# The last projection's first tiles are made during layer 3's last sums; a first mask, weights' wait, stage ends and first weights of attention at other places

## The chip, the cores and the metric

One core of a Trainium2 chip runs the whole program. The metric is the device time of one execution in microseconds; where several runs were made, their median. A profiled execution gives the trace that the times of single instructions come from.

A core has a TensorE for matrix products (PE; its weight loads are listed apart as PEld), a VectorE (DVE), a ScalarE (ACT), a GpSimd (POOL) and a SyncE (SP). Each engine works through its own list of instructions in a fixed order and waits on semaphores for the others. SP, POOL and ACT also issue DMAs, each in the order of its list: a DMA that has to wait for something holds up those behind it.

## The reference

Four graph layers on 2708 nodes with 512 features, each of the form x = layernorm(x + layer(x, adj)). adj is a symmetric 0/1 matrix with ones on its diagonal, about 2.3% full. Cut to what matters:

```python
def layer0(X, A):                      # at most 64 neighbours of each row
    Ab = A > 0
    keep = Ab & (jnp.cumsum(Ab, axis=1) <= 64)
    cnt = keep.sum(axis=1, keepdims=True)
    xj = leaky_relu((keep @ X / maximum(cnt, 1)) @ W_nb.T + b_nb)
    xi = leaky_relu(X @ W_line.T + b_line)
    return xi + where(cnt > 0, xj, 0)

def layer1(x, adj):
    agg = mask @ x / maximum(deg, 1)
    return relu(concat([x @ W_self + b_self, agg @ W_nb + b_nb]) @ W_comb + b_comb)

def heads(x, mask, W, a):              # 8 heads of 64, or one of 512
    Wh = einsum('nf,hfo->hno', x, W)
    e = leaky_relu((Wh @ a_src)[:, :, None] + (Wh @ a_dst)[:, None, :], 0.2)
    return softmax(where(mask, e, -9e15)) @ Wh

def layer2(x, adj): return heads(x, adj, W, a)          # 8 heads, side by side
def layer3(x, adj):
    x1 = elu(heads(x, adj, W1, a1))                     # 8 heads, side by side
    h2 = elu(heads(x1, adj, Wo, ao))                    # one head of 512
    return relu(h2 @ lin1_w + lin1_b) @ lin2_w + lin2_b
```

## The kernel before

The 2708 rows are NT = 22 tiles of 128 (the last has 20 rows); features are D = 512, so a product with a 512 x 512 weight is KD = 4 steps. The transposed adjacency matrix stays in SBUF as `maskT`, one byte an entry. Most pools are rings: a tile of a name takes the oldest of `bufs` buffers and waits until that one's readers are done. A scheduler orders each engine's instructions by priorities that follow the program text; `tc.issue_after(x)` asks for an instruction to be ordered behind x. `early(ahead, n, make)` makes item i a number of steps before it is used. `ahead`, `late` and `const` are pools that live through the whole fast path.

Stages, in their order, with the lines of the kernel before:

- Layer 0, projections (loop over t at L293 to L324). For each row tile: x is loaded and transposed (L125, L127), multiplied with W_nb (`keep_y`, L223 and L224, splits the product into two parts yH and yL) and with W_line (products at L229). The second one gets its bias (L318) and leaky relu and goes to r0_dram. Meanwhile HERE of the 22 row tiles of adj ("masks") are loaded (L242), counted by a Sigmoid (L247, ACT), scanned so that only 64 neighbours a row stay (`place`: L253 and L256, DVE) and turned (L265, PE) into maskT. The W_line weight is transposed before the loop (L137, L138).
- Layer 0, sums (the loop over blocks of four tiles with L459). 6 blocks of row tiles; each runs over 22 tiles j of y with two products a tile (yH, yL) against `kT`, the mask widened by ACT (L335). Generators are stepped between the products: `both`, once a step, makes the masks that are left (`other_masks`), the weights of layer 1 and small vectors of the attention layers; `todo`, on odd j, runs `finish` of the block before: bias, leaky relu, the addition of r0 and x (both loaded), layer norm, and the store to x1_dram (L384, POOL). A block ends with ACT's scaled copies `u<-acc` (L472).
- Layer 1: its projections (L478 to L491) and sums over the full mask (L505).
- Layers 2 and 3. `project` (products at L608) makes for each row tile R (the features scaled by `ecol`, L622), ucol, vcol and the row v, which goes to v_dram and comes back broadcast over all partitions (`v_bc`, L665). `heads_attention` then makes the sums: two blocks of 11 row tiles (1408 and 1300 columns), four pairs of heads a block, so 8 runs; each run has 22 steps j and each step, for its two heads, one DVE operation for e (L671, max(v, u) times mask), one ACT operation for c (L679, which says where the first branch holds) and PE's products po (L829) and, with c, pd (L744, the divisors). Products of the mask with `parts_m` (L727) belong to the divisors too: 88 for a block, in three portions, then `fold` (L716) and `keep` (L736). For block 0 all are run ahead of the first run; for block 1 during the run before it needs them.
- The output of a run of layer 2 is turned back (L777), copied into a tile `o` (L785) from the ring "xT", and stored to o_dram (L789, L791); layer 3's projection reads it again (`summed`), one tile ahead.
- The output of a run of layer 3 stays transposed and goes to oT_dram (L808); the reciprocals of its divisors are transposed after a block's last pair (`spread`: L795, L797) and stored to rc_dram by eight DMAs on POOL's queue (L799). The projection of the last head (`p4`, L608 again) takes its input from `elu_turned`: loads of oT (L880) and rc (L882), broadcast over the partitions, and then DVE (L884), ACT Exp (L885), DVE (L886, L887) for two tiles at a time; o lies in a part of `lin`, a large tile that is made when the attention's pools are given back.
- The last head's sums (L939 to L973) with the two linear layers, and the layer norm.

`okc` sums counts that must come to `expected`; otherwise a slower general version runs, which does not happen with these inputs.

Of the kernel before, what the change touches and what calls it, by code (L numbers as in the profile page):

```python
# [18 lines left out]
P = 128  # L19
# [11 lines left out]
def kernel(  # L31
# [18 lines left out]
    def rows(t):  # L50
        return min(P, N - t * P)
# [39 lines left out]
    oT_dram = dram.tile([D, N], F32, name="oT_dram")  # L91
    rc_dram = dram.tile([H, NT * P], F32, name="rc_dram")
# [102 lines left out]
    with ExitStack() as phase:  # L195
# [39 lines left out]
        HERE = NT - 7  # L235
# [40 lines left out]
        with ExitStack() as ph:  # L276
# [21 lines left out]
            for t in range(NT):  # L298
# [10 lines left out]
                now = counted < min(HERE, -(-t * HERE // (NT - 4)))  # L309
# [9 lines left out]
                low = leaky(u[:n], u[:n])  # L319
# [8 lines left out]
        with ExitStack() as ph:  # L328
# [9 lines left out]
            def other_masks():  # L338
# [9 lines left out]
                for i in range(HERE, NT):  # L348
# [9 lines left out]
                    for part in range(4):  # L358
                        place(i, m, places, part, 4)
                        yield  # L360
                    psum = (ps_mm.tile([P, G, P], BF16, name=f"pm{k % 2}") for k in range(3))
# [12 lines left out]
            def finish(ts_, us):  # L374
                for t in ts_:
                    n, u = rows(t), us[t]
                    r0, x0 = fetched(r0_dram, t, n), fetched(x, t, n)
# [4 lines left out]
                    nc.vector.tensor_add(u[:n], u[:n], x0)  # L382
# [66 lines left out]
            for i, b in enumerate(cuts):  # L449
                ts_ = range(*b)  # L450
                pa = {t: sums() for t in ts_}
                for j in range(NT):
# [9 lines left out]
                    if j % 2:  # L462
                        next(todo, None)
# [85 lines left out]
    expected = float(P * NT * (3 * H + 1))  # L549
# [10 lines left out]
    def project(name, source, layer, v_dram, cuts, turned=None):  # L560
# [12 lines left out]
        with ExitStack() as ph:  # L573
# [7 lines left out]
            if turned:  # L581
                twos = early(2, -(-NT // 2), lambda i: turned(sm, 2 * i, min(2 * i + 2, NT)))
                xTs = lambda t: twos(t // 2)[:, :, t % 2 * P:t % 2 * P + P]
            vrows, bs = {}, {}
# [14 lines left out]
            for t in range(NT):  # L599
# [19 lines left out]
                for a in range(2):  # L619
                    to, src = R2[:n, t, a * D // 2:(a + 1) * D // 2], pm[a][:n, :D // 2]  # L620
                    if heads > 1:
                        nc.vector.tensor_mul(to.rearrange("p (h o) -> p h o", h=hh),  # L622
# [19 lines left out]
            sq = sm.tile([P, NT, H], F32, name="sq", bufs=1)  # L642
            if heads < H:
                nc.vector.memset(sq, 0.0)
            dd = dcol[:, :, :heads]
            nc.vector.tensor_mul(sq[:, :, :heads], dd, dd)
            sq = sq.rearrange("p t h -> p (t h)")
# [36 lines left out]
    blocks = list(zip(cuts[:-1], cuts[1:]))  # L684

    def heads_attention(name, att, as_rows):
# [3 lines left out]
        with ExitStack() as ph:  # L690
# [56 lines left out]
            def finish(b, h0, p, pair, oT):  # L747
# [3 lines left out]
                feats, cols = slice(h0 * HO, (h0 + 2) * HO), slice(t0 * P, t0 * P + att.width(b))  # L751
# [41 lines left out]
                def spread():  # L793
                    ps = ps_t.tile([P, 512], F32, name="ps_t")
                    pe(nc.tensor.transpose(ps[:12 * H, :P], rcs[:, b].rearrange("p h t -> p (h t)"), ident))  # L795
                    r = sm.tile([12 * H, P], F32, name="r", bufs=1)
                    nc.scalar.copy(r, ps[:12 * H, :P])  # L797
                    for h in range(H):
                        nc.gpsimd.dma_start(rc_dram[h, t0 * P:t1 * P].rearrange("(t p) -> t p", p=P),  # L799
                                          r[12 * h:12 * h + nt])  # L800
# [6 lines left out]
                else:  # L807
                    nc.gpsimd.dma_start(oT_dram[feats, cols], oT.rearrange("p i c -> p (i c)")[:, :att.width(b)])  # L808
# [3 lines left out]

            products, fold, keep = masks(0, pd[1])
            for step in (*products, fold, keep):
                step()
            todo = {}
            for r, (b, h0) in enumerate(runs):
# [23 lines left out]
                todo = finish(b, h0, pd[r % 2], pair, oT)  # L841
# [31 lines left out]

    def elu_turned(sm, t0, t1):

        w = sum(rows(t) for t in range(t0, t1))
        cols = slice(t0 * P, t0 * P + w)
        o = lin[:, -KD * 1024:].rearrange("p (i k n) -> p i k n", i=4, k=KD)[:, t0 // 2 % 4]
        rc = sm.tile([P, KD, 2 * P], F32, name="rc2")
        nc.sync.dma_start(o[:, :, :w], oT_dram.rearrange("(k p) n -> p k n", p=P)[:, :, cols])  # L880
        for q in range(2):
# [460 lines left out]
```

## Time and profile before

| | us |
|---|---|
| three runs: lowest, median, highest | 3063.74, 3064.99, 3065.71 |
| profiled execution: its time | 3066.34 |
| profiled execution: span | 3064.6 |
| layer 0, projections | 0 to 217 |
| layer 0, sums | 217 to 504 |
| layer 1 | 504 to 945 |
| layer 2, projection and sums | to 1548 |
| layer 3, projection and sums | 1556 to 2228 |
| projection of the last head | 2255 to 2338 |
| its sums, linear layers, layer norm | to 3064.6 |

The mean granted TensorE clock is 0.986. In the profile, a line of a timeline has the start, the duration of the group, the engine, the line of the kernel, the operation, its output and inputs, their shapes, how often it ran, and in brackets the idle time ahead of it and what ended that. In a table of stretches, each row has a stretch's bounds and length, then for PE, PEld, DVE, ACT and POOL the busy time and the number of instructions, then the granted clock, the DMA's share and GB/s. This part of the page shows the span in 40 slices of 76.6 us, busy time in tenths:

```profile
PE   7999999999999999999998999999969999999997
DVE  5866649313234999999966999999943535344342
ACT  3556432113224899999955999999932000000001
PEclk9999999999999999999999999999989999999999
```

### The profile page before, as it was taken

To read this page: it belongs to the slowest core of one execution; us is meant where nothing else is said; L and a number is where in the kernel's file an instruction comes from. 1 tells how busy PE (TensorE), PEld (TensorE's weight loads), DVE (VectorE), ACT (ScalarE), POOL (GpSimd) and SP (SyncE) were. 2 spreads that over 40 slices of the span, in tenths; PEclk is the share of its full clock that TensorE was granted. 3 is DMA by queue.
4 is the path that set the end of the run, shared out by engine and by line. 5 is a ranking of instruction groups with operands and counts; after the bars stand their busy time and mean duration, and the time that the engine had idled before them with its cause. 6 is when DMAs were issued, how large, how long until landed. Compare 5 with 4: busy or idle time off the path is not lost. (4 is left out here: it accounts for less than half of the span.)

```text
span 3064.6 us, 36494 instructions
## 1 busy us (share of the span) xinstructions
PE 2918.2 (95%) x14456; PEld 1623.1 (53%) x14456; DVE 2021.9 (66%) x2408; ACT 1545.0 (50%) x1768; POOL 220.9 (7%) x354
## 2 busy tenths in 40 slices
PE   7999999999999999999998999999969999999997
PEld 4447676458887333444465333444356555555565
DVE  5866649313234999999966999999943535344342
ACT  3556432113224899999955999999932000000001
POOL 1110102101110000000022000000000000100001
PEclk9999999999999999999999999999989999999999
DMA  4542343322222000011044000000061000000000
GB/s 124 118 95 59 120 126 112 119 63 90 76 74 80 20 29 29 28 42 34 22 132 128 29 29 28 28 28 27 18 172 48 4 17 14 31 14 15 14 21 20
DMA packets 115972, 174.45 MB, mean 57 GB/s; under 512 B 40062, under 2 KB 63487, under 8 KB 115792
## 3 DMA queue, kind: packets, MB, share of 16 engines
q1 hardware_dynamic: 87120, 110.56, 12.1%
q0 software_dynamic: 18784, 57.79, 6.5%
q10 hardware_dynamic: 9888, 3.67, 0.5%
q8 instruction: 116, 1.90, 0.3%
q14 instruction: 64, 0.52, 0.1%
HBM read 142.01 MB, written 44.64 MB: 61 GB/s over the span
## 5 line engine op out<-in xcount | busy, mean ns | idle before, releaser
L671 DVE SCALAR_TENSOR_TENSOR e<-v_bc,ucol,maskT 128x1300 f32<-128x1300 f32 (+3 forms) x836 | 1181.8, 1474 | 336.7 <-PE pn L973 318.4
L679 ACT ACTIVATE c<-e,bcol 128x1300 fp8e4<-128x1300 f32 (+1 forms) x704 | 994.8, 1424 | 83.2 <-DVE e L671 33.2
L829 PE MATMUL po<-e,R 128*64 128x512 f32 (+2 forms) x4224 | 925.1, 548 | 30.7 <-DVE e L671 28.7
L829 PEld LDWEIGHTS po<-e,R 128*64 128x64 f32 x4224 | 348.6, 136 | 574.6 <-issue 383.7
L973 PE MATMUL pn<-e,R 128*128 128x512 f32 (+1 forms) x1056 | 413.4, 542 | 0.0
L973 PEld LDWEIGHTS pn<-e,R 128*128 128x128 f32 x1056 | 191.1, 190 | 199.2 <-issue 195.9
L941 ACT ACTIVATE w<-pl,b 128x256 f32<-128x256 f32 (+1 forms) x88 | 40.9, 465 | 373.4 <-PE pl L939 373.4
L459 PE MATMUL acc<-yH,kT 128*128 128x512 f32 x484 | 197.3, 408 | 4.3 <-ACT kT L335 4.3
L229 PE MATMUL pm<-w,xT 128*128 128x512 f32 (+1 forms) x384 | 178.7, 609 | 15.2 <-DVE yL L224 9.3
L459 PE MATMUL acc<-yL,kT 128*128 128x512 f32 x484 | 189.8, 392 | 0.0
L505 PE MATMUL acc<-yH,mf 128*128 128x512 f32 x484 | 188.4, 389 | 0.0
L505 PE MATMUL acc<-yL,mf 128*128 128x512 f32 x484 | 188.3, 389 | 0.0
L608 PE MATMUL pm<-w,xT 128*128 128x264 f32 (+1 forms) x704 | 169.5, 395 | 10.5 <-DVE R L622 5.1
L114 POOL TENSOR_TENSOR ln_rs<-ln_rs,half 128x1 f32<-128x1 f32 x88 | 59.2, 673 | 1569.7 <-DVE ln_rs L113 1563.8
L229 PE MATMUL pm<-weight,xT 128*128 128x512 f32 (+1 forms) x352 | 161.7, 602 | 5.9 <-DVE weight L138 5.2
L939 PE MATMUL pl<-lin 128*128 128x256 f32 (+1 forms) x704 | 154.8, 374 | 2.8 <-DVE lin L858 2.8
L948 PE MATMUL pl<-lin,w 128*128 128x512 f32 (+1 forms) x352 | 157.4, 592 | 0.0
L608 PEld LDWEIGHTS pm<-w,xT 128*128 128x128 f32 (+1 forms) x704 | 130.1, 190 | 38.5 <-issue 5.7
L939 PEld LDWEIGHTS pl<-lin 128*128 128x128 f32 x704 | 130.4, 192 | 33.7 <-issue 15.8
L502 ACT CAST mf<-maskT 128x1024 fp32r<-128x1024 fp8e4 (+1 forms) x66 | 64.4, 978 | 158.4 <-PE acc L505 147.9
L223 ACT CAST yH<-pm 128x512 fp32r<-128x512 f32 (+1 forms) x44 | 25.7, 585 | 230.2 <-PE pm L229 230.2
L335 ACT ACTIVATE kT<-maskT 128x512 fp32r<-128x512 fp8e4 (+1 forms) x132 | 77.6, 594 | 118.8 <-PE acc L459 118.7
(198 smaller groups left out, 2690.2 us busy)
## 6 DMA issues: line engine op xcount, KB each, us to landing
rows<-x_dram SPq DMA_DIRECT2D x63, 256.0 KB
v_bc<-v_dram SPq DMA_DIRECT2D x16, 704.0 KB
rows<-in_x_dram SPq DMA_DIRECT2D x42, 256.0 KB
x_dram<-u POOLq DMA_DIRECT2D x42, 256.0 KB, 2.3
v_bc<-v_dram SPq DMA_DIRECT2D x16, 650.0 KB
m<-in_adj_dram POOLq DMA_DIRECT2D x14, 677.0 KB, 6.7
r_dram<-u POOLq DMA_DIRECT2D x21, 256.0 KB, 2.3
rows<-r_dram SPq DMA_DIRECT2D x21, 256.0 KB
```

The costliest lines, as they stand in the source:

```text
L229: order(nc.tensor.matmul(pm[:n], xT[:, k, :n], w[:, k, :], start=(k == 0), stop=(k == KD - 1)))
L335: made = nc.scalar.activation(kT[:, :w], maskT[:, j, b[0] * P:b[0] * P + w], AF.Relu, scale=-1.0)
L459: nc.tensor.matmul(pa[t], kT[:, (t - b[0]) * P:(t - b[0] + 1) * P], y[:, j, :], start=(j == 0 and y is yH), stop=(j == NT - 1 and y is yL))
L502: nc.scalar.copy(mf[:, :g1 - g0, :], maskT[:, g0:g1, t * P:(t + 1) * P])
L505: nc.tensor.matmul(pa, mf[:, j - g0, :], y[:, j, :], start=(j == 0 and y is yH), stop=(j == NT - 1 and y is yL))
L608: nc.tensor.matmul(pm[a][:n, :D // 2 + heads], xT[:, k, :n], w[:, k, a, :D // 2 + heads], start=(k == 0), stop=(k == KD - 1))
L671: nc.vector.scalar_tensor_tensor(e[:, :w], v[:, :w], ucol[:, j, h:h + 1], maskT[:, j, c0:c0 + w], op0=OP.max, op1=OP.mult)
L679: nc.scalar.activation(c[:, :w], e[:, :w], AF.Sigmoid, bias=bcol[:, j, h:h + 1], scale=STEP, saturate=False)
L829: pe(nc.tensor.matmul(po[i][HO * k:HO * k + HO, :c1 - c0], R2[:, j, h * HO:(h + 1) * HO], e[:, c0:c1], start=(j == 0), stop=(j == NT - 1)))
L939: nc.tensor.matmul(pl[:, :w], self.lin1[:, k, f * P:(f + 1) * P], h[:, k, :w], start=(k == 0), stop=(k == KD - 1))
L948: nc.tensor.matmul(pl[:n], gT[:, f, (t - t0) * P:(t - t0) * P + n], self.lin2[:, f, :], start=(f == 0), stop=(f == KF - 1))
L973: nc.tensor.matmul(pn[k][:, :w], R2[:, j, k * P:(k + 1) * P], e[:, :w], start=(j == 0), stop=(j == NT - 1))
```

## The change

- Layer 0, projections: HERE is 14 instead of 15, and the first mask is counted at t = 2 instead of t = 1. x is added to the leaky relu's result right there, before it is stored to r0_dram.
- Layer 0, sums: a mask waits two more steps between its scan and its turn; `finish` no longer loads and adds x; its steps run at two of three j instead of at every second.
- `project`: the last layer's input tiles are cut into three single tiles and then pairs; `sq` holds only the heads that there are; it returns the scaling (L622) of tile 20.
- `heads_attention`: the e's of the first three steps of run 0 are ordered behind that scaling; block 0's products with parts_m, their fold and keep move into run 0 (at j = 12, 16, 20) and to the first steps of run 1.
- The last run's output tiles `o` come from the ring "e" instead of "xT"; `r` comes from the ring "spare".
- oT_dram and rc_dram become one buffer for each block.
- During the last run of layer 3 (in the program's text at j = 9, 13 and 17; the scheduler puts the parts where their inputs allow) `elu_turned` makes tiles 0, 1 and 2 for the last projection, in buffers of the rings "rows", "xT" and "spare". The loads of `elu_turned` are ordered one behind the other.

```diff
-        HERE = NT - 7
+        HERE = NT - 8
...
-                now = counted < min(HERE, -(-t * HERE // (NT - 4)))
+                now = counted < min(HERE, -(-(t - 1) * HERE // (NT - 5)))
...
-                low = leaky(u[:n], u[:n])
+                leaky(u[:n], u[:n])
+                low = nc.vector.tensor_add(u[:n], u[:n], xs(t))
                 nc.gpsimd.dma_start(r0_dram[t * P:t * P + n, :], u[:n])
...
                         place(i, m, places, part, 4)
                         yield
+                    yield
+                    yield
...
-                    r0, x0 = fetched(r0_dram, t, n), fetched(x, t, n)
+                    r0 = fetched(r0_dram, t, n)
...
-                    nc.vector.tensor_add(u[:n], u[:n], x0)
...
-                    if j % 2:
+                    if j % 3:
                         next(todo, None)
...
             if turned:
-                twos = early(2, -(-NT // 2), lambda i: turned(sm, 2 * i, min(2 * i + 2, NT)))
-                xTs = lambda t: twos(t // 2)[:, :, t % 2 * P:t % 2 * P + P]
+                cuts_ = [(t, t + 1) for t in range(3)] + [(t, min(t + 2, NT)) for t in range(3, NT, 2)]
+                parts = early(2, len(cuts_), lambda i: ready[i] if i in ready else turned(sm, *cuts_[i]))
+                xTs = lambda t: parts(t if t < 3 else (t - 3) // 2 + 3)[:, :, ((t - 3) % 2 if t > 2 else 0) * P:][:, :, :P]
...
-                        nc.vector.tensor_mul(to.rearrange("p (h o) -> p h o", h=hh),
+                        scaled[t] = nc.vector.tensor_mul(to.rearrange("p (h o) -> p h o", h=hh),
...
+            return scaled.get(NT - 2)
...
-                    o = ahead.tile([P, KD, P], F32, name="xT")
+                    o = (att.pool.tile([P, att.W], F32, name="e", bufs=5)[:, :KD * P].rearrange("p (t c) -> p t c", t=KD)
+                         if last else ahead.tile([P, KD, P], F32, name="xT"))
...
-                    r = sm.tile([12 * H, P], F32, name="r", bufs=1)
+                    r = late.tile([P, D], F32, name="spare", bufs=2)[:12 * H, :P]
...
-                        nc.gpsimd.dma_start(rc_dram[h, t0 * P:t1 * P].rearrange("(t p) -> t p", p=P),
+                        nc.gpsimd.dma_start(rc_dram[b][h].rearrange("(t p) -> t p", p=P),
...
-                    nc.gpsimd.dma_start(oT_dram[feats, cols], oT.rearrange("p i c -> p (i c)")[:, :att.width(b)])
+                    nc.gpsimd.dma_start(oT_dram[b][feats, :w], oT.rearrange("p i c -> p (i c)")[:, :w])
...
             products, fold, keep = masks(0, pd[1])
-            for step in (*products, fold, keep):
-                step()
-            todo = {}
+            todo = {12: products[:1], 16: products[1:2], 20: products[2:], NT: [fold], NT + 2: [keep]}
...
+                if r + 1 == len(runs):
+                    for j, steps in meanwhile.items():
+                        todo[j] = todo.get(j, []) + steps
                 for j in range(NT):
-                    es = [att.weights(b, h, j, v) for h, v in zip(hs, vs)]
+                    with tc.issue_after(scaled.ins) if r == 0 and j < 3 else nullcontext():
+                        es = [att.weights(b, h, j, v) for h, v in zip(hs, vs)]
...
+    loads, ready = [], {}
+
     def elu_turned(sm, t0, t1):
+        if t0 < 3:
+            o = ahead.tile([P, D], F32, name="rows", bufs=3).rearrange("p (k n) -> p k n", k=KD)
+            rc = (ahead.tile([P, KD, P], F32, name="xT") if t0 < 2 else
+                  late.tile([P, D], F32, name="spare", bufs=2).rearrange("p (k n) -> p k n", k=KD))
+        else:
+            o = lin[:, -KD * 1024:].rearrange("p (i k n) -> p i k n", i=4, k=KD)[:, t0 // 2 % 4]
+            rc = sm.tile([P, KD, 2 * P], F32, name="rc2")
+        for b, (a, z) in enumerate(blocks):
+            c0, c1 = max(a, t0), min(z, t1)
+            if c0 < c1:
+                w = sum(rows(t) for t in range(c0, c1))
+                to, cols = slice((c0 - t0) * P, (c0 - t0) * P + w), slice((c0 - a) * P, (c0 - a) * P + w)
+                with tc.issue_after(loads[-1].ins) if loads else nullcontext():
+                    loads.append(nc.sync.dma_start(
+                        o[:, :, to], oT_dram[b].rearrange("(k p) n -> p k n", p=P)[:, :, cols]))
+                for q in range(2):
+                    with tc.issue_after(loads[-1].ins):
+                        loads.append(nc.sync.dma_start(
+                            rc[HO * q:HO * q + HO, :, to],
+                            rc_dram[b].rearrange("(k q) n -> q k n", q=2)[q, :, cols].partition_broadcast(HO)))
...
-            project(f"p{2 + i}", source, i, vd[i], blocks)
-            heads_attention(f"a{2 + i}", att, i == 0)
+            scaled = project(f"p{2 + i}", source, i, vd[i], blocks)
+            heads_attention(f"a{2 + i}", att, i == 0, scaled, {
+                9 + 4 * t: [lambda t=t: ready.update({t: elu_turned(None, t, t + 1)})] for t in range(3)} if i else {})
```

More of the change, by code (lines that the diff above doesn't have):

```diff
@@ L1 @@
-from contextlib import ExitStack
+from contextlib import ExitStack, nullcontext
 from itertools import chain
@@ L90 @@
     o_dram = dram.tile([N, D], F32, name="o_dram")
-    oT_dram = dram.tile([D, N], F32, name="oT_dram")
-    rc_dram = dram.tile([H, NT * P], F32, name="rc_dram")
+    oT_dram, rc_dram = [], []
     behind = []
@@ L548 @@
     nc.vector.tensor_scalar(rdeg, iso, 0.0, None, op0=OP.is_equal, op1=OP.add, accum_out=okc[:, 3:4])
-    expected = float(P * NT * (3 * H + 1))
+    expected = float(P * NT * (2 * H + 2))
     def split(pool, dst, src):
@@ L581, in project @@
             if turned:
-                twos = early(2, -(-NT // 2), lambda i: turned(sm, 2 * i, min(2 * i + 2, NT)))
-                xTs = lambda t: twos(t // 2)[:, :, t % 2 * P:t % 2 * P + P]
-            vrows, bs = {}, {}
+                cuts_ = [(t, t + 1) for t in range(3)] + [(t, min(t + 2, NT)) for t in range(3, NT, 2)]
+                parts = early(2, len(cuts_), lambda i: ready[i] if i in ready else turned(sm, *cuts_[i]))
+                xTs = lambda t: parts(t if t < 3 else (t - 3) // 2 + 3)[:, :, ((t - 3) % 2 if t > 2 else 0) * P:][:, :, :P]
+            vrows, bs, scaled = {}, {}, {}
             def keep_v(t):
@@ L641, in project @@
             keep_v(NT - 1)
-            sq = sm.tile([P, NT, H], F32, name="sq", bufs=1)
-            if heads < H:
-                nc.vector.memset(sq, 0.0)
+            sq = sm.tile([P, NT * H], F32, name="sq", bufs=1)[:, :NT * heads]
             dd = dcol[:, :, :heads]
-            nc.vector.tensor_mul(sq[:, :, :heads], dd, dd)
-            sq = sq.rearrange("p t h -> p (t h)")
+            nc.vector.tensor_mul(sq.rearrange("p (t h) -> p t h", h=heads), dd, dd)
             nc.vector.tensor_scalar(sq, sq, RANGE * RANGE, None, op0=OP.is_le, op1=OP.add,
                                     accum_out=okc[:, layer:layer + 1])
+            return scaled.get(NT - 2)
     class Weights:
@@ L684, with heads_attention @@
     blocks = list(zip(cuts[:-1], cuts[1:]))
-    def heads_attention(name, att, as_rows):
+    for i, (a, z) in enumerate(blocks):
+        oT_dram.append(dram.tile([D, (z - a) * P], F32, name=f"oT_dram{i}"))
+        rc_dram.append(dram.tile([H, (z - a) * P], F32, name=f"rc_dram{i}"))
+    def heads_attention(name, att, as_rows, scaled, meanwhile={}):
         with ExitStack() as ph:
@@ L745, in divisors, with finish @@
                                                 start=(j == 0 and h == hs[0]), stop=(j == NT - 1 and h == hs[1])))
-            def finish(b, h0, p, pair, oT):
+            def finish(b, h0, p, pair, oT, last):
                 t0, t1 = att.blocks[b]
                 nt = t1 - t0
-                feats, cols = slice(h0 * HO, (h0 + 2) * HO), slice(t0 * P, t0 * P + att.width(b))
+                feats, w = slice(h0 * HO, (h0 + 2) * HO), att.width(b)
                 got = {}
@@ L840, in heads_attention @@
                 late_steps = {j: todo[j] for j in todo if j >= NT}
-                todo = finish(b, h0, pd[r % 2], pair, oT)
+                todo = finish(b, h0, pd[r % 2], pair, oT, r + 1 == len(runs))
                 for j, steps in late_steps.items():
@@ L872, in summed @@
         return o
+    loads, ready = [], {}
     def elu_turned(sm, t0, t1):
-        w = sum(rows(t) for t in range(t0, t1))
[L877 to L881, printed above, removed]
-            nc.sync.dma_start(rc[HO * q:HO * q + HO, :, :w],
-                                rc_dram.rearrange("(k q) n -> q k n", q=2)[q, :, cols].partition_broadcast(HO))
+        if t0 < 3:
[18 more added lines that the diff above has]
+                            rc_dram[b].rearrange("(k q) n -> q k n", q=2)[q, :, cols].partition_broadcast(HO)))
+        w = sum(rows(t) for t in range(t0, t1))
         nc.vector.tensor_mul(o[:, :, :w], o[:, :, :w], rc[:, :, :w])
```

## The prediction

> **What bounds the kernel now.** I read the totals first, then the waits of the TensorE, then the hand-overs between stages in the timeline. The totals: busy time, share of the span, instructions.
>
> ```profile
> PE 2918.2 (95%) x14456; PEld 1623.1 (53%) x14456; DVE 2021.9 (66%) x2408; ACT 1545.0 (50%) x1768; POOL 220.9 (7%) x354
> ```
>
> PE is busy for 2918.2 of 3064.6 us, so 146.4 us of idle time are all that an edit can win which, like this one, takes no product away (what a lowered clock adds comes on top). Where those sit, by what PE waited for (total, times, longest):
>
> ```profile
> PE po L829 <- DVE e L671: 28.7, 69, 0.5
> PE pm L608 <- DVE lin L887: 23.7, 1, 23.7
> PE pm L229 <- DVE yL L224: 9.3, 11, 1.6
> PE ps_v L593 <- DVE b L615: 6.4, 4, 5.0
> PE pm L265 <- DVE spare L256: 6.0, 4, 2.4
> PE pm L229 <- ACT xT L127: 5.8, 2, 5.1
> PE pm L229 <- DVE weight L138: 5.2, 1, 5.2
> PE pm L608 <- issue: 4.6, 1, 4.6
> PE pd L727 <- DVE parts_m L556: 3.3, 1, 3.3
> ```
>
> One wait of 23.7 us and half a dozen of 3 to 6 us; the rest is crumbs. But PE isn't alone in bounding. In two stages the DVE is full (stretch, then busy time of PE, PEld, DVE, ACT, POOL, then clock): layer 0's projections and the sums of layer 3.
>
> ```profile
> 46.00:194.00 148.00, 139.83 (x631) 72.25 (x629) 134.55 (x117) 85.44 (x115) 17.10 (x28) 1.00 0.51 110
> 1690.00:2226.00 536.00, 517.55 (x3574) 214.13 (x3564) 527.35 (x377) 494.17 (x372) 7.87 (x15) 1.00 0.07 27
> ```
>
> There an added DVE operation is paid for, and the change adds some to both. I take it in the order of the run.
>
> **Layer 0, projections.** Three edits. The first mask's scan no longer stands in front of the last weight copy:
>
> ```profile
> 29.05 2.98 DVE L253 TENSOR_TENSOR_SCAN places<-m,over 128x1354 bf16<-128x1354 bf16 x1 [1.66 <-ACT m L247]
> 32.66 3.90 PE L229 MATMUL pm<-weight,xT 128*128 128x512 f32 x5 [5.16 <-DVE weight L138]
> ```
>
> The wait shrinks from 5.16 us by the scan plus the 1.66 us that the DVE waited for it, less what overlapped: −4.3. One mask fewer is turned here: −1.5 (a turn at L265 takes PE 1.49 us). Against them stands u += x, 22 operations of 0.68 us (the duration of the same operation at L382). A tile with a mask keeps the DVE 9.33 us (from the span between two like tiles) and PE 8.83 (7.41 of products and the turn); so on 14 tiles the DVE already leads, and the 9.3 us behind L224 say the same. 0.6 us of DVE occupancy on 14 tiles is 8.4; tiles without a mask have slack that gives some back. Nothing if hidden, 15.0 (22 × 0.68) if never; I take +6. The loads of x need the buffer that the sum now holds longer: they are ahead by some 5 us and I cost that at nothing; without the cover it is the added 0.7 us a tile. Together +0.2.
>
> **Layer 0, sums.** Two more steps between scan and turn aim at the waits behind L256, 6.0 + 1.8 us; I take 6 of 7.8. The mask moved here costs its turn, 1.5, and 0.6 for a wait like the 4.3/6 behind L335. The x loads (22 of 256 KB) and 22 sums leave, off PE's path. Net −4 (bounds −5.7 to +2).
>
> **Layer 0 to layer 1.** ScalarE holds both xT and the fourth scaled sum, and that sum's buffer waits for the store of the last block:
>
> ```profile
> 508.29 0.69 ACT L472 ACTIVATE u<-acc,rkeep 128x512 f32<-128x512 f32 x1 [4.22 <-DMA x_dram<-u]
> 509.51 2.08 PE L229 MATMUL pm<-w,xT 128*128 128x512 f32 x2 [5.08 <-ACT xT L127]
> ```
>
> Steps on 14 of 22 positions instead of 11, and lighter ones, store it several positions (1.6 us of products each and more) earlier: −4.2. After the pause eight products took 5.70 us instead of 8 × 0.592 = 4.74; I count −0.8 of that. −5 (bounds −6 to 0).
>
> **Layer 2, into its sums.** The first e's (1.69 us each) and ScalarE's function changes no longer intrude in the projection (eight tiles took 35.2 us, 32.9 at the undisturbed 4.11): −2.3. The 88 mask products (5.15 us) and the 3.27 us wait ahead of them go from the start into the first run. But the e's they covered are then late: the sums wait for the DVE instead, by e number eight −3 rather than −8. A block-0 run with such products took 74.06 us against 71.7, the one after it 65.75 against 66.95: +1.2 to +2.4 given back. Net −1.5 (−4 to +2).
>
> **Layer 2 to layer 3.** The last three output tiles wait for the xT ring, which their own stores hold:
>
> ```profile
> 1554.80 0.52 ACT L785 COPY xT<-ps_t 128x256 f32<-128x256 f32 x2 [2.23 <-DMA o_dram<-xT]
> 1556.26 2.10 PE L608 MATMUL pm<-w,xT 128*128 128x264 f32 x4 [4.62 <-issue]
> ```
>
> From another ring, L785 runs 2 to 4 us earlier and xT of tile 0 with it. On SP's queue all four stores now stand ahead of the second o load, which then goes at about its present time, so tile 1 isn't helped. −3.5 of the 4.62 and the slow clock behind it (0 to −7).
>
> **Layer 3, into its sums.** Early e's stand in the DVE's queue waiting for v_bc, and the projection's small work behind them:
>
> ```profile
> 1635.94 0.37 PE L593 MATMUL ps_v<-ident,b 128*8 128x128 f32 x1 [5.04 <-DVE b L615]
> ```
>
> With a second pause of 1.53 us it is 6.6 us, and five tiles took 30.7 us instead of 5 × 4.7. The e's now queue behind the scaling of tile 20, so −6.6, −1.7 at the start of the sums as in layer 2, +1.3 for the products in the run: −7 (−10 to −3).
>
> **Layer 3 to layer 4**, half of the change's worth. Now everything is serial: the last products end at 2228.08, reciprocals, eight stores to rc_dram until 2243, loads, elu, and only then:
>
> ```profile
> 2231.89 3.51 POOL L799 DMA_DIRECT2D rc_dram<-r  x7 [2.13 <-ACT r L797]
> 2244.03 13.84 SPq L882 DMA_DIRECT2D rc<-rc_dram  x8
> 2254.96 7.26 PE L608 MATMUL pm<-w,lin 128*128 128x257 f32 x26 [23.66 <-DVE lin L887]
> ```
>
> With oT_dram and rc_dram split by block, tiles 0 to 2 need block 0 alone, are made during block 1's runs, and can start at 2228.1. 22 tiles took 82.7 us to 2337.7; less 1.4 for the cold start (8.56 us for a pair instead of 7.15) and 1.7 waiting for R, 3.62 a tile. Three take 10.9; L795 stands among them in PE's order and waits 1.4 for the reciprocals: 2240.4. The pair (3,4) needs lin's space (2228.2), its rc2 buffer (about 2233, behind the last oT store), a shared DMA, and 4.4 us of DVE and ScalarE: ready about 2244, a stall of 3.5, and 1.0 for the clock behind a pause (0.96 in the eight products above). Then 19 × 3.62 + 1.7: 2315.5. −22.2.
>
> The inserts cost something: three tiles of three operations at 128x512 are (1.23 + 0.69 + 1.23)/2 = 1.6 us each by the pairs' rows, 4.8 in the full DVE. It waits 6.8 us at run borders in this stretch, and the pieces stand there: +2.4 (0 to 4.8). On ScalarE three exponentials of 0.55 and six function loads of 1.28 are 9.4 us; it is idle 536 − 494 = 42, five a run, so each hole of 3.1 is made up within the run. If not, e's buffers run out and the DVE waits. Layer 3 to 4 is −19.8 (−24 to −10).
>
> In this trace the function load at 2250.42 takes 1.28 us and the Exp starts at 2251.71, with no gap between. The Trainium skill (ScalarE: Activation LUTs, "What ACT_TABLE_LOAD costs") speaks against the change: it adds a drain to each switch of function sets, about 2.66 us in all. By it ScalarE's part would be an estimated 17.6 us instead of 9.4 and the term some 3 to 5 us worse; the row decides.
>
> **Sum:** 0.2 − 4 − 5 − 1.5 − 3.5 − 7 − 19.8 = −40.6. The profiled execution took 3066.34 with a span of 3064.6, so it would be 3025.7; it lies 1.35 above the median of the runs, 3064.99, and I forecast 3024.4. The memset, the constant and the move of r touch nothing that waits: 0, or 0.5 us once.
>
> **Rivals.**
> (a) The stall before tile 3 stays long. For it: the 2 MB of lin1 and four lin loads go out at 2228 to 2229 together, and rc's loads took 5 us to the first DVE operation (2244.03 to 2249.12). If the pair is ready only at 2254.4 as now, PE wins just the three tiles, 10.9, less 2.4 of inserts: −8.5 in place of −19.8, 3036.
> (b) Layer 0's projection is bound by the DVE throughout, +15 instead of +6, and the mask turns wait as before (−4 becomes +2): 3064.99 − 40.6 + 9 + 6 = 3039. Against it: DVE idles 13.4 us in 46 to 194.
> (c) The early tiles are made early in name only: L608 of tile 0 still waits behind PSUM or the reciprocals. −19.8 becomes +2.4: 3047. Against: it follows the last product directly in PE's order.
> (d) Slower: a piece of elu blocks the DVE's queue. Each L884 stands ahead of e's and waits for loads from rc_dram, written by the queue whose eighth store waited 6.76 us, and which stand on SP's queue ahead of v_bc's loads. If DVE stands 16 us at each of three places (48 us), the gain is gone: 3072. It decides once the wait passes 13.5 us each. Against: a run lasts 67 us and block 0's rc is out a third into run 4.
>
> **Chances.** Forecast 0.64, (a) 0.15, (b) 0.09, (c) 0.04, (d) 0.05, all gains cancelling 0.03. A measurement of this kernel can tell about 0.2%, 6 us: faster 0.92, same 0.03, slower 0.05. The likeliest case's own range adds the terms' bounds in part: 3012 to 3035. Up to (a), (b) and (c), and down to all bounds' better half: 3009 to 3044.
>
> **What would show it.** Right: the wait behind L887 is under 8 us and L608 of layer 4 starts within 2 us of the last L744; no wait over 2 us at L593; the pause ahead of layer 1 under 2 us; first weights by 29 us. Wrong: DVE idle behind a load of rc in layer 3's sums; waits behind L224 grown by more than 8 us; v_bc loads late.

## The result, and the profile after

The changed kernel takes 3026.73 us (median of 4 runs, 3025.22 to 3028.63), the kernel before 3064.36 (median of 4, 3061.36 to 3065.71): a ratio of 0.9879, 95% interval 0.9862 to 0.9896. The profiled execution's span fell from 3064.6 to 3023.9 us, by 40.7; the medians differ by 37.6. The forecast was 3024.4 us, in a range of 3012 to 3035.

The totals, and what PE now waits for (total, times, longest):

```profile
PE 2908.5 (96%) x14456; PEld 1616.0 (53%) x14456; DVE 2023.5 (67%) x2417; ACT 1533.0 (51%) x1764; POOL 222.4 (7%) x354
```

```profile
PE po L839 <- DVE e L672: 28.2, 68, 0.7
PE pm L228 <- DVE yL L223: 18.5, 16, 2.0
PE ps_v L596 <- DVE b L618: 9.0, 6, 6.1
...
PE po L839 <- DVE ue L638: 4.3, 1, 4.3
PE po L839 <- DVE R L625: 4.2, 1, 4.2
...
PE pm L611 <- DVE lin L913: 2.6, 1, 2.6
```

(L672, L839 and L223 here are L671, L829 and L224 before; L255 was L256, L596 was L593, L611 was L608, L618 was L615, L732 was L727, L749 was L744, L802 was L795, L906 was L882, L910 to L913 were L884 to L887.) The wait of 23.7 us is gone, and those ahead of layer 1, layer 3's first product and the first W_line product are gone or under 1 us. Three are new or larger: yL (9.3 to 18.5, of which 16.7 in layer 0's projections and 1.8 in layer 1's), the start of both layers' sums (4.3 and 4.2, where the products with parts_m waited 3.3 and 3.2 before), and a pause of 6.1 + 2.6 us in the last projection. PE is also busy 9.7 us less with the same 14456 products, and the mean clock rose from 0.986 to 0.993.

From the first and last start of each stage's products, stage by stage (a stage runs to the start of the next one; one execution of each kernel, bounds to 0.1 us):

| stage | before | after | difference | forecast |
|---|---|---|---|---|
| layer 0, projections | 221.4 | 223.6 | +2.2 | +0.2 |
| layer 0, sums | 281.8 | 279.1 | −2.7 | −4 |
| pause and layer 1's projection | 168.6 | 166.8 | −1.8 | −5 |
| layer 1, sums | 220.8 | 220.9 | +0.1 | 0 |
| layer 2, to its last po | 654.4 | 650.2 | −4.2 | −1.5 |
| layer 2 to 3 | 9.3 | 4.0 | −5.3 | −3.5 |
| layer 3, to its last po, with the inserts | 670.6 | 661.7 | −8.9 | −4.6 |
| layer 3 to 4 and the last projection | 110.4 | 91.2 | −19.2 | −22.2 |
| the rest | 727.3 | 726.4 | −0.9 | 0 |

No stage moved against its forecast, but that the sum came out so close is luck, since its errors cancel: the first three lines won 6.5 us less than forecast, the three of layers 2 and 3 won 8.8 more, the last projection 3 less (and that was its shortest execution, see below). That is what the experiments have to explain.

The timeline at the first W_line product, and at the start of the last projection (start, duration, engine, line, operation, idle time ahead):

```profile
27.00 3.70 PE L228 MATMUL pm<-weight,xT 128*128 128x512 f32 x8 [0.78 <-DVE weight L137]
```

```profile
2206.61 0.82 PE L749 MATMUL pd<-c,parts_c 128*12 128x384 fp8e4 x16
2207.36 1.13 PE L611 MATMUL pm<-w,rows 128*128 128x257 f32 x4
...
2213.11 1.43 SPq L906 DMA_DIRECT2D rc<-rc_dram  x2
...
2223.77 1.23 DVE L910 TENSOR_TENSOR lin<-lin,rc 128x1024 f32<-128x1024 f32 x1 [8.13 <-DMA rc<-rc_dram]
2224.92 0.15 DVE L618 TENSOR_SCALAR b<-pm 128x1 f32<-128x1 f32 x1
...
2225.21 0.37 PE L596 MATMUL ps_v<-ident,b 128*1 128x128 f32 x1 [6.08 <-DVE b L618]
...
2228.22 6.05 PE L611 MATMUL pm<-w,lin 128*128 128x257 f32 x20 [2.64 <-DVE lin L913]
```

The early tiles do what they should: PE goes from the last divisor product straight to tile 0. Then the pair of tiles 3 and 4 is late: its rc load, issued at 2213.11, lets the DVE go on only at 2223.77. And while the DVE waits at L910, the small operation behind it in its queue (L618, the b of tile 2) waits too, so PE's first pause is booked under L596 and not under lin.

### The profile page after: what moved, and what is told of

The parts are those of the page before. It is cut to its first block, busy times and chain, and to the rows that moved or that the text cites. A ratio compares the mean times of both kernels' runs of the same rounds, so it can differ in the third digit from the quotient of the medians.

```text
span 3023.9 us, 36506 instructions
## 1 busy us (share of the span) xinstructions
PE 2908.5 (96%) x14456; PEld 1616.0 (53%) x14456; DVE 2023.5 (67%) x2417; ACT 1533.0 (51%) x1764; POOL 222.4 (7%) x354
## 4 chain that ended last, share of the span: by engine, by line
PE 62%; DVE 15%; issue 14%; ACT 4%; DMA 3%; POOL 1%; SPq 0%; DVEq 0%; POOLq 0%; ACTq 0%
PE pn L999 13%; PE po L839 12%; DVE e L672 9%; PE acc L506 7%; PE pm L228 6%; PE pm L611 5%; PE pl L974 5%; PE pl L965 5%; PE acc L460 4%; ACT c L680 3%; PE pd L749 2%; PE ps_tr L124 1%; DVE maskT L485 1%; DMA rows<-o_dram 1%; DVE places L252 0%
## 5 line engine op out<-in xcount | busy, mean ns | idle before, releaser
L672 DVE SCALAR_TENSOR_TENSOR e<-v_bc,ucol,maskT 128x1300 f32<-128x1300 f32 (+3 forms) x836 | 1184.7, 1479 | 322.4 <-PE pn L999 314.1
L839 PE MATMUL po<-e,R 128*64 128x512 f32 (+2 forms) x4224 | 925.2, 550 | 38.4 <-DVE e L672 28.2
L839 PEld LDWEIGHTS po<-e,R 128*64 128x64 f32 x4224 | 348.6, 137 | 582.1 <-issue 387.6
L228 PE MATMUL pm<-w,xT 128*128 128x512 f32 (+1 forms) x384 | 181.0, 616 | 21.9 <-DVE yL L223 18.5
L611 PE MATMUL pm<-w,xT 128*128 128x264 f32 (+1 forms) x704 | 165.3, 388 | 4.0 <-DVE R L625 3.0
L611 PEld LDWEIGHTS pm<-w,xT 128*128 128x128 f32 (+1 forms) x704 | 127.3, 186 | 29.6 <-ACT xT L126 5.6
L228 PEld LDWEIGHTS pm<-w,xT 128*128 128x128 f32 (+1 forms) x384 | 72.1, 192 | 122.1 <-issue 101.0
```

Source lines behind the costliest of these rows:

```text
L228: order(nc.tensor.matmul(pm[:n], xT[:, k, :n], w[:, k, :], start=(k == 0), stop=(k == KD - 1)))
L611: nc.tensor.matmul(pm[a][:n, :D // 2 + heads], xT[:, k, :n], w[:, k, a, :D // 2 + heads], start=(k == 0), stop=(k == KD - 1))
L672: nc.vector.scalar_tensor_tensor(e[:, :w], v[:, :w], ucol[:, j, h:h + 1], maskT[:, j, c0:c0 + w], op0=OP.max, op1=OP.mult)
L839: pe(nc.tensor.matmul(po[i][HO * k:HO * k + HO, :c1 - c0], R2[:, j, h * HO:(h + 1) * HO], e[:, c0:c1], start=(j == 0), stop=(j == NT - 1)))
```

## The experiments

All are edits of the changed kernel. Those without an interval are read by stage, since most stages that an edit doesn't touch repeat well: in six other executions with the same code there, layer 0's sums took 278.7 to 279.0 us and layer 2 to 3 took 4.0; only layer 0's projections (223.0 to 226.5 in eight executions), layer 3 (661.4 to 664.5) and the last projection (91.2 to 94.0) differ by some us without an edit there. No run undoes the first mask's new place, the mask fewer or the finish's steps at two of three j alone.

### x added in the finish again (e1)

```diff
-                leaky(u[:n], u[:n])
-                low = nc.vector.tensor_add(u[:n], u[:n], xs(t))
+                low = leaky(u[:n], u[:n])
...
-                    r0 = fetched(r0_dram, t, n)
+                    r0, x0 = fetched(r0_dram, t, n), fetched(x, t, n)
...
+                    nc.vector.tensor_add(u[:n], u[:n], x0)
                     layer_norm(sm, u[:n], n, u[:n])
```

> The changed kernel, but x is again loaded and added in the finish of layer 0's sums. Theory (layer 0's projections run at the pace of the DVE, each added operation is paid): the waits for yL fall from 15.7 us in 30 to 217 us to about 9, layer 0's sums begin 7 to 8 us earlier than at 223.6, and since the finish of a block is off PE's path the end comes 5 to 8 us earlier than the 3023.9 us span of the changed kernel. Rival (the loss comes from the masks' new places, not from the addition): the waits for yL stay above 14 and the sums begin within 2 us of 223.6.

Span 3017.1, time 3018.92 us (3065.88 for the kernel before, beside it). The sums begin at 214.4 instead of 223.6. PE's waits for yL in 30 to 214 us, in the changed kernel and in e1:

```profile
PE pm L228 <- DVE yL L223: 15.7, 13, 2.0
```

```profile
PE pm L228 <- DVE yL L223: 9.9, 11, 1.6
```

The theory holds. Three later kernels with x in the finish began them at 214.0, 215.5 and 218.5: on average 215.6 for the four against 224.4 for the eight with the addition on the DVE in the loop, so the addition costs about 9 us: more than the forecast's +6, about the 8.4 that it would be if each of 14 mask tiles paid its 0.6 us.

### x added on GpSimd (e10)

```diff
-                leaky(u[:n], u[:n])
-                low = nc.vector.tensor_add(u[:n], u[:n], xs(t))
+                low = leaky(u[:n], u[:n])
+                nc.gpsimd.tensor_add(u[:n], u[:n], xs(t))
```

> The changed kernel with u += x in layer 0's projections on GpSimd instead of the DVE. Theory (the DVE sets the pace there and GpSimd, busy 11% of that time, is free): as with x added in the finish, the waits for yL fall to about 9 us and the sums begin 7 to 9 us earlier than at 223.6, but the pause of 10.3 us ahead of layer 1 that the kernel with x in the finish had doesn't come back (under 3 us), so the span is 7 to 9 us shorter. Rival (GpSimd is slow and holds its queue, so masks and rows come late, or it slows the DVE's scans): the sums begin within 2 us of 223.6 or later.

The pause of 10.3 us named there was a misreading: with x in the finish layer 1's first product starts at 495.5, 2.0 us behind the start of the last sum. Here the sums begin at 225.4, and the span is 3030.0: the rival. The timeline of this kernel in the loop shows why:

```profile
65.83 3.03 DVE L252 TENSOR_TENSOR_SCAN places<-m,places,over 128x1354 bf16<-128x1354 bf16 x1
66.00 3.92 POOL L319 TENSOR_TENSOR u<-u,rows 128x512 f32<-128x512 f32 x1 [4.67 <-DVE u L186]
68.90 1.75 DVE L255 TENSOR_TENSOR m<-m,places 128x1354 bf16<-128x1354 bf16 x1
...
93.61 1.26 POOL L319 TENSOR_TENSOR u<-u,rows 128x512 f32<-128x512 f32 x1 [1.13 <-DVE u L186]
```

The groups of the DVE in 46 to 194 us, first of the kernel with the addition on GpSimd, then of the changed kernel (busy time, mean ns):

```profile
L255 DVE TENSOR_TENSOR m<-m,places 128x1354 bf16<-128x1354 bf16 (+1 forms) x25 | 30.7, 1229 | 0.5
```

```profile
L255 DVE TENSOR_TENSOR m<-m,places 128x1354 bf16<-128x1354 bf16 (+1 forms) x27 | 23.1, 857 | 0.2
L319 DVE TENSOR_TENSOR u<-u,rows 128x512 f32<-128x512 f32 x15 | 10.3, 690 | 0.4
```

The mean of the DVE's multiplication goes from 857 to 1229 ns: 25 × 0.37 = 9.3 us, nearly all that the DVE was spared. The single instructions show how. An addition takes GpSimd 1.25 to 1.28 us where the DVE runs nothing beside it (8 of the 22), against 0.69 on the DVE. The 14 others start some 0.17 us into a scan and take 3.9 us: they end about 1.06 us behind the scan, as if they had waited for it. The multiplication that follows the scan starts while the addition still runs and takes 1.27 to 1.75 us; the ones with no addition beside them take 0.84 to 0.87, as in the changed kernel. The Trainium skill (SBUF — State Buffer, "SBUF: two separate sides") says that GpSimd and a DVE operation with two SBUF inputs lock a shared pair of ports against each other, and that whichever starts first has it for its whole instruction. The trace agrees: scan, addition and multiplication behave as if they took turns, and the scan, which starts first, stays at 3.0 us.

### Two extra steps taken out (e5)

```diff
                         place(i, m, places, part, 4)
                         yield
-                    yield
-                    yield
```

> The changed kernel without the two steps between a mask's last scan and its turn in layer 0's sums. Theory (the steps remove the waits behind L255 but push the vectors of the attention layers into layer 1's projection): the waits are back with 6 to 8 us in 217 to 504 us, and layer 1's projection (504.7 to 669.0) gets 1.5 to 2.5 us shorter, since the DVE has less to do there: net +3 to +6. Rival (the waits were covered by the mask's other new place): span within 2 us.

PE's waits in layer 0's sums without the steps:

```profile
PE pm L264 <- DVE spare L255: 1.8, 1, 1.8
PE pm L264 <- DVE w L255: 1.0, 1, 1.0
```

Only 2.8 of the 7.8 us come back, and the stage is shorter: 277.1 instead of 279.1 us; layer 1's projection, from its first product to its first sum, takes 160.8 instead of 162.6 to 164.8. Span 3018.5. Neither theory nor rival had it this way round: in this kernel the steps lose some 4 us. Three later kernels (e12 to e14) have x back in the finish and no steps. Their sums take 284 us, with 5.9 us of waits behind L255 in e12:

```profile
PE pm L264 <- DVE w L255: 5.7, 5, 1.8
PE pm L264 <- DVE spare L255: 0.2, 1, 0.2
```

e1, with x in the finish and the steps, has none of these waits, and its sums took 279.1. So either edit covers the waits: the steps all of them, the lighter finish alone the larger part (2.8 are left of 5.9). With the heavy finish the steps win 5 us in the sums, but 3.6 of them are given back in layer 1's projection (166.4 us in e1, 162.8 in e12, the granted clock 0.99 in both); from the first sum of layer 0 to the first of layer 1 e1 takes 447.5 us, e12 to e14 449.4 to 450.6. With the light finish the steps lose more than they win. What they push back are operations for the attention layers' vectors: in layer 1's projection the DVE has some 27 of them in the changed kernel and in e1, none in e5 and e12. In the changed kernel, 505 to 669 us:

```profile
L444 DVE TENSOR_REDUCE wa<-spare 128x1 f32<-128x512 f32 (+1 forms) x14 | 9.4, 684 | 0.0
L443 DVE TENSOR_TENSOR spare<-spare 128x512 f32<-128x512 f32 x13 | 9.0, 691 | 1.5 <-DMA spare<-in_L_gnn_Wo_dram 1.5
```

What exactly the steps delay in layer 0's sums beside a wait of 2.1 us for a weight of layer 1 stays open.

### Products and first e's, each undone alone (e2, e7)

```diff
-            todo = {12: products[:1], 16: products[1:2], 20: products[2:], NT: [fold], NT + 2: [keep]}
+            for step in (*products, fold, keep):
+                step()
+            todo = {}
```

> The changed kernel, but block 0's 88 products with parts_m, their fold and keep run ahead of the first run again, in both layers; the first e's stay behind the projection. Theory (the products cover a DVE that is late anyway, so that moving them wins only part of their 5.15 us): each layer's sums end 1 to 3 us later than in the changed kernel, 2 to 6 us in all, and the wait of 4.3 us ahead of the first po turns into one ahead of the products. Rival (moving the products is the whole gain there): 4 to 5 us a layer, 8 to 10 in all.

```diff
-                    with tc.issue_after(scaled.ins) if r == 0 and j < 3 else nullcontext():
+                    with tc.issue_after(scaled.ins) if False else nullcontext():
```

> The changed kernel without the order that keeps the first three steps' e's behind the scaling of tile 20; block 0's products stay inside run 0. Theory (both parts work apart: early e's stop the projection's small work, the products' place sets what the first run waits for): layer 3's projection has its waits behind b (L618) of 5 to 7 us back and takes some 6 us longer, layer 2's 2 us; but the first e's are then made early and the wait of 4.3 us ahead of the first po shrinks to under 2 in both layers: net +1 to +5. Rival (the order is worth nothing once the products are inside the run, since the sums' start is bound by the e's in either case): span within 2 us or shorter.

With the kernel before and the changed one this makes a square (us from the first product of a layer's projection to its last po; layer 3 before has no elu inserts):

| | layer 2 | layer 3 |
|---|---|---|
| neither (before) | 654.4 | 670.6 |
| e's ordered, products first (e2) | 655.5 | 668.3 |
| e's free, products inside run 0 (e7) | 646.5 | 663.1 |
| both (changed) | 650.2 | 661.7 |

The product move is the gain: −5.3 and −6.6 with the order, −7.9 and −7.5 without it (in layer 3 with the inserts' cost inside). For e2 the rival was nearer, and even it was too low: span 3035.7, 11.8 more. With the e's ordered behind the projection and the products first, the wait ahead of them grows from 3.3 to 6.1 us, as the DVE does e's meanwhile:

```profile
PE pd L732 <- DVE parts_m L557: 6.1, 1, 6.1
```

For e7 the rival holds: span 3024.2. But the order isn't neutral; its two effects cancel. In layer 2 it keeps 2.6 us of disturbance out of the projection (92.0 to 89.4) and costs 6.3 behind it, most of that at the start of the sums, where PE waits 4.3 + 1.2 us instead of 1.5 + 1.4 and then runs at a lower clock. Stretches of 16 us across that start, in the changed kernel and in e7 (busy times, then the clock):

```profile
980.00:996.00 16.00, 10.38 (x41) 3.58 (x40) 15.62 (x34) 13.77 (x15) 1.62 (x2) 0.89 0.13 27
```

```profile
983.00:999.00 16.00, 13.84 (x64) 5.04 (x62) 15.33 (x33) 10.03 (x12) 0.75 (x2) 1.00 0.31 69
```

In layer 3, where the free e's stop the projection for 5.8 us, the two cancel to within what layer 3 varies by. Other executions repeat this: layer 2 takes 649.9 to 650.8 us in the eight with the order and the products in the run, 646.5 to 647.7 in the four without the order (e7, e12 to e14). So the order is a loss of some 3 us there and no gain in layer 3 (661.2 to 663.1 us without it in e7, e12 and e13).

### The last output tiles in the ring xT (e3)

```diff
-                         if last else ahead.tile([P, KD, P], F32, name="xT"))
+                         if False else ahead.tile([P, KD, P], F32, name="xT"))
```

> The changed kernel, but the last output tiles of layer 2 come from the ring xT again. Theory (these tiles' stores hold the ring that tile 0's xT needs): the wait of 4 to 5 us ahead of layer 3's first product is back, from the last po of layer 2 to that product it is about 9 us as in the kernel before (1547.0 to 1556.3) instead of 4.0 (1540.6 to 1544.6), and the span grows by 4 to 6 us. Rival (the gain there came from the earlier e's and the order of the loads): it stays below 6 us.

```profile
1549.70 0.52 ACT L792 COPY xT<-ps_t 128x256 f32<-128x256 f32 x2 [2.58 <-DMA o_dram<-xT]
...
1551.30 1.22 PE L611 MATMUL pm<-w,xT 128*128 128x264 f32 x2 [5.10 <-issue]
```

From the last po (1541.6) to this product it is 9.7 us, against 4.0: the theory, and the whole of the 5.3 us that this stage won. The span is 3034.3, more than the 4 to 6 us that were expected; of the 10.4 us more, 5.7 are here, and some 2 each in layer 0's projections, layer 3 and the last projection, the stages that differ anyway.

### The split by block alone, and the early tiles (e9, e4)

In e9 the input tiles of the last projection are made in pairs in lin and rc2, none early:

```diff
-                cuts_ = [(t, t + 1) for t in range(3)] + [(t, min(t + 2, NT)) for t in range(3, NT, 2)]
...
+                twos = early(2, -(-NT // 2), lambda i: turned(sm, 2 * i, min(2 * i + 2, NT)))
+                xTs = lambda t: twos(t // 2)[:, :, t % 2 * P:t % 2 * P + P]
...
-        if t0 < 3:
+        if t0 < 0:
...
-                9 + 4 * t: [lambda t=t: ready.update({t: elu_turned(None, t, t + 1)})] for t in range(3)} if i else {})
+                9 + 4 * t: [lambda t=t: ready.update({t: elu_turned(None, t, t + 1)})] for t in range(3)} if False else {})
```

> The changed kernel, with oT_dram and rc_dram split by block, but the last projection's input tiles made in pairs in lin and rc2 as in the kernel before, none of them early. Theory (the early tiles fill the time in which the pair in lin is loaded, and win 11 to 14 us; the split wins the rest): after the last pd product PE waits 13 to 17 us for the first pair instead of starting at once, the projection ends 11 to 14 us after its last product later than in the changed kernel (90.2 us from the last po to its last L611 product), less 2 to 3 us of DVE work that layer 3's sums get back: span +8 to +12. Rival (the split is all, early tiles only move the wait): span within 3 us.

```profile
PE pm L610 <- DMA rc<-rc_dram: 20.7, 1, 20.7
```

Span 3037.3, 13.4 more: the theory, at more than its 8 to 12. The split alone wins little here: PE still waits 20.7 us for the first pair, more than the 13 to 17 expected (with lin1's 2 MB in flight, see e11). From the last po to the last product of the projection it is 110.4 before, 105.8 with the split, 91.2 with the early tiles. Layer 3 takes 659.4, 2.0 to 5.1 less than with the inserts (661.4 to 664.5); 2.4 was the forecast.

e4 has only the last line of that diff, so that the tiles keep their buffers.

> The changed kernel, but tiles 0 to 2 of the last projection aren't made during the last runs: elu makes them at the projection's start, in the same buffers, from the split oT_dram and rc_dram. Theory A (making them early is what is worth 11 to 14 us; the split by block is only its condition): the DVE and ScalarE can't begin before the last e and c, so the first product starts 5 to 9 us after the last pd product instead of at once, and the pair behind comes later too: span +6 to +12. Theory B (the split by block is what counts, since their loads land early in either case): the first product starts within 4 us and the span grows by 0 to 4, since the DVE's 4.8 us in the full attention come back. Theory C (loads aren't issued early either, the wait is back): +20.

Span 3022.3, and no answer to its question: without being told, the scheduler put tiles 0 and 1 in the same places among the e's (L910 on them at 2000.7 us), since nothing but their inputs and buffers holds them back. Only tile 2 moved, into the projection, where PE waits 1.1 us for it. So what lets tiles 0 and 1 be early here is their buffers outside the attention's pools, not the place in the text.

### lin1's load later (e11)

```diff
     last = Last(ph4, "", lin, ahead)
-    last.load()
+    with tc.issue_after(stored[1].ins):
+        last.load()
```

(`stored[1]` is the last rc_dram store of block 1, on the same queue.)

> The changed kernel with the 2 MB load of lin1 behind the eight rc_dram stores on POOL's queue instead of ahead of them. Theory (the pause of 6.1 + 2.6 us behind tile 2 in the last projection is the rc load of tiles 3 and 4, which shares the DMA engines with those 2 MB): rc lands within 5 us of its issue (2213.11) instead of 10.7, the pause falls to 3 to 5 us, and the projection ends 4 to 6 us earlier after the last po than the 91.2 us of the changed kernel. Rival (the load is late because its own descriptors are slow and lin's four loads are in front of it): the pause stays above 7 us.

```profile
2211.94 1.24 SPq L906 DMA_DIRECT2D rc<-rc_dram  x2
...
2217.79 1.23 DVE L910 TENSOR_TENSOR lin<-lin,rc 128x1024 f32<-128x1024 f32 x1 [3.05 <-DMA rc<-rc_dram]
...
2222.23 9.62 PE L611 MATMUL pm<-w,lin 128*128 128x257 f32 x32 [2.74 <-DVE lin L913]
```

Stretches of 13 us across the pause (busy times, then the clock), in the changed kernel and in e11:

```profile
2219.00:2232.00 13.00, 4.28 (x14) 3.24 (x13) 5.16 (x7) 3.50 (x8) 0.51 (x1) 0.74 0.91 187
```

```profile
2219.00:2232.00 13.00, 10.00 (x34) 7.89 (x34) 4.70 (x9) 3.50 (x8) 0.00 (x0) 0.74 1.06 289
```

The load now lets the DVE go on 5.9 us after its issue instead of 10.7 (9.7 in e4, 13.8 in e9), and the pause falls from 8.7 to 1.0 + 2.7: the 2 MB were its cause (7.9 + 2.6 against 2.8 + 2.7 us in e12 and e13, which differ by this edit alone). But the end moves by 0.8 us only, not by the 4 to 6 expected (90.4 from the last po against 91.2; 91.4 to 94 in other executions). The 32 products behind the pause take 9.62 us where an undisturbed pair takes 7.2, the clock being 0.74 in 2219 to 2232, as it was without this edit, and for the next pair the DVE waits 6.1 us for rc. The time isn't in the one transfer; the loads of the first pairs take turns at being late. The 2 MB are issued at 2214.35 here and may be what delays the next pair; a still later place wasn't tried.

### Several parts together (e12 to e14)

e12 undoes the addition, the steps and the order on the e's; e13 also has lin1 later; e14 also a fourth early tile.

> The changed kernel with three of its parts undone: x is added in the finish of layer 0's sums, no extra steps between scan and turn, no order on the first e's. By the single runs: 3023.9 - 6.8 - 5.4 and 0 to -2.5: span 3009 to 3012, time 3011 to 3014 us. Rival (the first two are one gain, since both come from the DVE work in layers 0 and 1): 3016 to 3019.

> As the kernel before this one in the call, and lin1's load behind the rc_dram stores. If the pause in the last projection is lin1's, 3 to 6 us less than that kernel; if not, the same within 2.

> As the kernel before this one in the call, and a fourth tile of the last projection made early, in the ring xT. If the pause behind the early tiles is longer than 1.6 us (the DVE's price of a tile), the fourth tile's 3.6 us fill it: 1 to 2 us less; if the pause is gone, 1 to 2 us more.

| | us (4 runs) | ratio to before | 95% |
|---|---|---|---|
| changed kernel | 3026.73 | 0.9879 | 0.9862 to 0.9896 |
| e12 | 3021.24 | 0.9849 | 0.9825 to 0.9872 |
| e13 | 3020.97 | 0.9851 | 0.9827 to 0.9874 |
| e14 | 3022.90 | 0.9863 | 0.9837 to 0.9889 |

e12 missed its 3011 to 3014, and the rival's 3016 to 3019 too: as shown above, the steps that lose 4 to 6 us with the light finish win 2 to 3 with the heavy one, so two of its single gains exclude each other. e13 and e14 are e12 within the noise; the fourth tile shortens the last projection (90.6 us from the last po, 93.1 in e13), and layer 3 took 664.5 instead of 662.5. All three have lower ratios than the changed kernel, but the intervals overlap. e1's 3018.92 has no interval. That one of them beats the changed kernel isn't shown by their times; what is shown is the 9 us of the addition and the 3 us of the order, each in its own stage.

## Why the prediction was right, and where its terms were off

**What bounds the kernel** was right: PE's waits were the store to draw from, and the number of products stayed the same. Of the signs named, the first weights (27.0), the first product of the last projection (0.75 us behind the start of the last L749 group) and the waits at L596 in layers 2 and 3 (at most 0.8) came as said. The wait behind L913 is under 8 us only because 6.1 of the 8.7 us stand under L596. And one sign of being wrong showed, if barely: the waits for yL grew by 9.2 us (7.4 of them in layer 0's projections), where more than 8 was to count; the addition's term below is what it points at.

**Layer 0, projections.** The first weights came 5.7 us earlier (32.66 to 27.00; 4.3 forecast). The addition was mis-sized: the step "tiles without a mask have slack that gives some back" brought +6; it measured 9, nothing was given back. (The stage's own +2.2 is one execution; the others with this code lie between +1.6 and +5.1.)

**Layer 0, sums.** "Two more steps aim at the waits" was half of it. The waits went, and the steps alone can remove them (e1), but taking x out of the finish, which the prediction booked as off PE's path, had already covered most; in this kernel the steps cost about 2 us there.

**Pause ahead of layer 1.** Its −4.2 was right in size (6.3 to 2.0 us from the last sum to the first product), though no run undoes the steps at two of three j alone; with x in the finish the pause is 2.0 us in e1 and 2.4 to 3.5 in e12 to e14. The clock's share was read too small: the first eight products took 3.70 us, not 5.70, because undisturbed products start 0.43 us apart, though each is listed with 0.592, so that eight don't take 8 × 0.592. What failed is that nothing was booked behind it: the attention layers' vectors, pushed back by the added steps, run in layer 1's projection, whose products wait 1.8 us for yL. At a granted clock of 1.00 that projection took 162.6 to 163.3 us in six executions with them and 160.8 in e5 without; at 0.99 it took 164.8 in this execution, 162.3 before.

**Layers 2 and 3, into their sums.** The step "+1.2 to +2.4 given back" by the products inside the run was too dear, and the e's order was taken for the gain. (Layer 2's terms, −2.3, −3 and +1.2 to +2.4, also add up to −2.9 to −4.1 and not to the −1.5 that was booked.) In a run that waits for the DVE, PE's extra products cost almost nothing: the square shows −5 to −8 a layer, where the 88 products alone are 5.15 us. For the order it shows +3.7 in layer 2 and nothing clear in layer 3.

**Layer 2 to 3.** The mechanism was right, and the size lay between the forecast −3.5 and its bound: −5.3.

**Layer 3 to 4.** Tiles 0 to 2 at once and L795 among them: right. The inserts cost layer 3 2.0 to 5.1 us (+2.4 forecast). The stall before tile 3 was mis-sized: 3.5 us forecast, 6.1 + 2.6 measured. That is rival (a) in its mechanism, shared DMA with lin1's 2 MB, at 3 of its 11.3 us. Rival (d) did not show: no L910 stood waiting in layer 3's sums, and v_bc's waits (3.7 us) were no longer than before (4.4).

**ScalarE's function loads**, at a switch in layer 3's sums:

```profile
2006.00 1.28 ACT L911 ACT_TABLE_LOAD   x1
2007.30 0.63 ACT L911 ACTIVATE xT<-rows 128x512 f32<-128x512 f32 x1
2007.94 1.28 ACT L680 ACT_TABLE_LOAD   x1
2009.24 1.38 ACT L680 ACTIVATE c<-e,bcol 128x1300 fp8e4<-128x1300 f32 x1
```

Two switches and the exponential take 3.2 us; each load follows the instruction before it at once, so the row was the right price. The 2.66 us a switch of the Trainium skill (ScalarE: Activation LUTs, "What ACT_TABLE_LOAD costs") don't show here.

## What to carry to other kernels

Work that a full engine covers is nearly free on the other one: moving PE's products under DVE-bound steps won 5 to 8 us a layer, while 22 additions of 0.69 us moved into a DVE-bound loop cost 9 us. Making the first tiles of a stage early pays only until the next tile is due, so its transfers have to be counted with everything that is issued at the same moment, and an operation that waits for one of them also holds the small ones behind it in its queue. And edits that cover the same wait should be tried alone and together: here either one covers most of the wait, and the steps on top of the lighter finish are a loss.

## What was not expected of the hardware

GpSimd's addition of 128x512 f32 took 1.26 us alone and 3.92 beside a DVE scan, and the DVE's multiplication behind that scan up to 1.75 us instead of 0.86. A pause of 4.3 us at the start of the sums took the mean clock to 0.89 over 16 us, where without it it was 1.00. And layer 0's projections, with the same code, took 223.0 to 226.5 us in seven executions, while the sums behind them repeated within 0.4 us.
